# Softmax denominators summed by accumulating transfers between SBUF tiles, with two products with ones per unit in place of twelve

## The chip, the cores and the metric

One core of one Trainium2 chip. The metric is the device time of one execution in microseconds; "time" is the median of several executions, and "span" is the length of the one execution that was profiled.

In the profile PE is TensorE (the products), ACT ScalarE (here the exp and copies), DVE VectorE and POOL GpSimd (element by element; GpSimd also issues the accumulating transfers), SP the queue that issues most other transfers. A transfer **lands** when it is complete; the time to landing is counted from the start of its issue. SBUF holds the tiles, PSUM the results of products, HBM is the memory outside the core.

## The reference, cut to what matters

Eight images of 256 channels and 32 x 32 pixels go through a convolution-and-attention layer (layer 0), a channel attention and a layer of experts (layer 1). The change touches the softmax of layer 0: for each image and each of 8 heads, 1024 queries of 32 channels attend to 1426 pooled keys.

```python
# q: (8, 8 heads, 1024, 32); k, v: (8, 8 heads, 1426, 32); all float32
attn = jax.nn.softmax(jnp.einsum('bhqd,bhkd->bhqk', q_g, k) * SCALE, axis=-1)
out_att = jnp.einsum('bhqk,bhkd->bhqd', attn, v)
# ... mixing, projection, residual; then the second layer:
t = t + _L1_attn_ref(_ln_t(t), ...)
t = t + _L1_ffn_ref(_ln_t(t), ...)      # 8 experts, three matmuls each
```

## The kernel before: the parts that matter

The keys lie on the partitions: 1426 keys are eleven chunks of 128 and one of 18. A **unit** is one image, one half of the heads (four) and one half of the queries (512); there are 32. A unit has twelve **steps**, one per chunk: scores into PSUM, exp into an SBUF tile `pt` of 128 x 2048, then two groups of four products, one with the values and one with a matrix of ones, which gives the sum over the keys.

```python
def scores(b, c, sl, kc):
    ...
    pt = T(work, [P, 4, 512], "pt", bufs=2)
    f.act.activation(pt[:w], t[:w], AF.Exp, scale=SCALE0)
    return pt

def values(b, c, kc, pt, pv):
    w = KEY_CHUNKS[kc][1]
    for what in range(2):                      # 0: values, 1: ones
        for j in range(4):
            h = 4 * c + j
            lhsT = kit.ones[:w, :DH] if what else vts[b][kc // 4][:w, kc % 4, h * DH : (h + 1) * DH]
            f.pe.matmul(pv[DH * j : DH * j + DH, what, :], lhsT=lhsT, rhs=pt[:w, j, :],
                        start=kc == 0, stop=kc == NKC - 1)
```

All other work of the two attentions (convolutions, keys and values of the next image, the second layer's attention of earlier images) is written as generators, here called threads, and put between the steps. A model of each engine's clock decides at build time which thread goes next; on the chip every engine then runs in a fixed order. `PACE` is the TensorE time that background may take per step.

```python
for i in range(len(steps) + 1):
    if i < len(steps):
        ...
        pt = scores(b, c, sl, kc)
        f.step()
    if late is not None:
        ...
        values(b1, c1, kc1, pt1, pv)
        if kc1 == NKC - 1:
            ...                                # copy out, spawn normalise and project
    if i < len(steps):
        late = b, c, sl, kc, pt
        f.step(PACE)                           # 2.8 us of background
f.finish(5)
```

Of the kernel before, what the change touches and what calls it, by code (L numbers as in the profile page):

```python
# [16 lines left out]
P = 128  # L17
# [8 lines left out]
NE = 8  # L26
SCALE0 = DH ** -0.5
SCALE1 = C ** -0.5
PACE = 2.8
MARGIN = 1.5  # L30
AHEAD = {"DVE": 6.0, "ACT": 1.0, "POOL": 4.0, "SP": 10.0}
BUFS = {"sm": 2}
LIMIT = 1e12
# [610 lines left out]
class Flow:  # L644
# [18 lines left out]
    def __init__(self, tc, kit):  # L663
        nc = tc.nc
        self.tc, self.kit = tc, kit
        self.now = dict.fromkeys(("PE", "DVE", "ACT", "POOL", "SP"), 0.0)
        self.last = {}
        self.ready, self.read, self.writer, self.rings = {}, {}, {}, {}
        self.pe = self.Engine(self, "PE", nc.tensor)
        self.ve = self.Engine(self, "DVE", nc.vector)  # L670
        self.act = self.Engine(self, "ACT", nc.scalar)
        self.pool = self.Engine(self, "POOL", nc.gpsimd)
        self.sp = self.Engine(self, "SP", nc.sync)
        self.threads = []
        self.credit = 0.0

    def tile(self, pool, shape, tag, bufs=1):
        t = self.kit.tile(pool, shape, tag, bufs=bufs)
        ring = self.rings.setdefault(tag, [])
        self.ready[t.name] = self.end(ring[-bufs]) if len(ring) >= bufs else 0.0  # L680
        ring.append(t.name)
        return t

    def end(self, name):
        return max(self.ready.get(name, 0.0), self.read.get(name, 0.0))

    def free(self, tag, bufs=1):
        ring = self.rings.get(tag, [])
        return self.end(ring[-bufs]) if len(ring) >= bufs else 0.0

    def cost(self, engine, op, out, ins):
# [7 lines left out]
        if "dma" in op:  # L699
            return 0.1  # L700
# [18 lines left out]
    def note(self, engine, op, ins, args, kwargs):  # L719
# [18 lines left out]
        cost = self.cost(engine, op, out, srcs)  # L738
        self.now[engine] = end = start + cost
        lag = 3.0 if "dma" in op else 0.15  # L740
        self.ready[o] = max(self.ready.get(o, 0.0), end + lag)
        self.writer[o] = engine
# [17 lines left out]
    def runnable(self, need):  # L760
# [5 lines left out]
        if tag is not None:  # L766
            at = max(at, self.free(tag, BUFS[tag]))
        if engine == "PE":
            return not self.closed and self.credit > 0 and at + MARGIN <= pe
# [9 lines left out]
    def step(self, pace=None):  # L779
# [3 lines left out]
        if pace is not None:  # L783
            self.credit = min(self.credit + pace, 3 * pace)
# [6 lines left out]
    def finish(self, rank):  # L791

        while any(t[2] <= rank for t in self.threads):
            self.credit, self.closed = 1.0, False
            ready = [t for t in self.threads if self.runnable(t[1])]
            self.resume((ready or [t for t in self.threads if t[1][0] is not None])[0])


def attention(tc, kit, nb, x, t1, t2, hn, bounds, vecs, q_t, kv_t, proj_t, gqk_t, wqk, wqkv, vecs1, w1_d, w1c, gate_d, wrc):
# [7 lines left out]
    with ExitStack() as ctx:  # L807
# [48 lines left out]
        for t in bounds:  # L856
            f.pool.memset(t, 0.0)

# [4 lines left out]
        def mix():  # L863
# [53 lines left out]
            bd = T(wp, [P, 2, P], "bd")  # L917
# [12 lines left out]
            bdt = T(wp, [P, 2, P], "bdt")  # L930
# [26 lines left out]
        ks, qs, vts = {}, {}, {}  # L957

# [15 lines left out]
        def maps(xp, todo, done, freed):  # L974

            for m in (2, 3, 0, 1):
                c = m % 2
                yield until(lambda: len(done) >= len(todo) - 1)
                p = T(work, [P, NK], "p", bufs=2)
# [12 lines left out]
                yield until(lambda: len(todo) < 2 + 2 * len(freed))  # L992
                yield pool(p)
                acc = T(work, [P, NK], "acc", bufs=2)
                for s, n in enumerate(SIDES):
                    o = OFFS[s]
                    f.pool.tensor_scalar(
                        acc[:, o : o + n * n],
                        p[:, o : o + n * n],
                        mid[:, c * 4 + s : c * 4 + s + 1],  # L1000
                        db(c, s),
                        ALU.mult,
                        ALU.add,
                    )
                todo.append((c, p, acc))

        def convolve(todo, done):

            for m in range(4):
# [67 lines left out]
        def prepare(b, todo, done, freed):  # L1077
# [57 lines left out]
            t5 = T(work, [P, 2, 32, 5], "pool5")  # L1135
# [13 lines left out]
            yield from maps(xp, todo, done, freed)  # L1149

            for c in range(2):
                yield until(lambda: c == 0 or turn[0] >= 2 * b - 1)
                q = qs[b, c] = T(work, [P, HW], "q", bufs=3)
                for half in range(2):
# [11 lines left out]
                    f.act.activation(q[:, sl], ps, AF.Copy, scale=vec[:, V_NW + c : V_NW + c + 1])  # L1166

        def keys_and_values(b, done, freed):
            yield until(lambda: len(done) == 2)
            vts[b] = []  # L1170
            for k0 in range(0, NKC, 4):
                vt = T(work, [P, 4, C], "vt", bufs=6)
                yield from by_tokens(done[:2], vt, k0)
                vts[b].append(vt)
            freed.append(True)

            yield until(lambda: len(done) == 4)
            for k0 in range(0, NKC, 4):
                kt = T(work, [P, 4, C], "kt")
                yield from by_tokens(done[2:], kt, k0)  # L1180
                s0, w = KEY_SLICES[k0 // 4]
                for c in range(2):
                    if k0 == 0:
                        yield until(lambda: c == 0 or turn[0] >= 2 * b - 1)
# [6 lines left out]

        def ahead(b):
            todo, done, freed = [], [], []
            f.spawn(keys_and_values(b, done, freed), 1)
            f.spawn(convolve(todo, done), 2)
            f.spawn(prepare(b, todo, done, freed), 3)

        def scores(b, c, sl, kc):
# [5 lines left out]
            pt = T(work, [P, 4, 512], "pt", bufs=2)  # L1204
# [3 lines left out]
        def values(b, c, kc, pt, pv):  # L1208
            w = KEY_CHUNKS[kc][1]
            for what in range(2):  # L1210
                for j in range(4):
                    h = 4 * c + j
                    lhsT = kit.ones[:w, :DH] if what else vts[b][kc // 4][:w, kc % 4, h * DH : (h + 1) * DH]
                    f.pe.matmul(
                        pv[DH * j : DH * j + DH, what, :],
                        lhsT=lhsT,
                        rhs=pt[:w, j, :],
                        start=kc == 0,
                        stop=kc == NKC - 1,
                    )  # L1220

        def normalise(b, c, sl, av):
            yield ve(av)
            rec = T(work, [P, 512], "rec")
            f.ve.reciprocal(rec, av[:, 1, :])
            yield pool(rec)
            f.pool.tensor_tensor(atts[b, c][:, sl], av[:, 0, :], rec, ALU.mult)
            for o in (0, C):
                f.pool.tensor_tensor(hi, hi, av[:, 1, o : o + C], ALU.add)
            for o in (0, C):  # L1230
                f.pool.tensor_tensor(lo, lo, rec[:, o : o + C], ALU.add)

        def project(b):
            yield until(lambda: scored[0] >= b - 1)
            t = T(work, [P, 2, HW], "t", bufs=2)
            f.sp.dma_start(t, x[b].rearrange("(k p) n -> p k n", p=P))
            for m in range(2):
                for half in range(2):
                    sl = slice(half * 512, half * 512 + 512)
                    yield pe(atts[b, 0], atts[b, 1], tag="sm")  # L1240
# [5 lines left out]
                    yield ve(ps, t)  # L1246
                    f.ve.scalar_tensor_tensor(t[:, m, sl], ps, bias[:, m : m + 1], t[:, m, sl], ALU.add, ALU.add)
            f.sp.dma_start(t1[b], t)
            tokens.append(t)
# [36 lines left out]
        turn, scored, written, tokens, probabilities = [0], [0], [0], [], []  # L1286

        def layer1():

            for b in range(nb):  # L1290
                yield until(lambda: len(tokens) > b)
                t = tokens[b]
# [13 lines left out]
                for n in range(4):  # L1306
# [15 lines left out]
                    yield until(lambda: 4 * b + n < written[0] + 2)  # L1322
                    p1 = T(work, [P, 8, C], "p1", bufs=2)
                    for g in range(4):
                        yield pe(y, tag="sm")
                        ps = small()
                        for u in range(2):
# [9 lines left out]
                        f.act.activation(  # L1337
                            p1[:, 2 * g : 2 * g + 2, :], ps.rearrange("p (u c) -> p u c", u=2), AF.Exp, scale=SCALE1
                        )
                    probabilities.append((b, q, p1, v))  # L1340
                scored[0] += 1

        def outputs():

            for i in range(4 * nb):
                yield until(lambda: len(probabilities) > i)
                b, q, p1, v = probabilities[i]
                res = T(work, [P, 2, C], "res", bufs=2)
                f.sp.dma_start(res, t1[b][:, :, q])
                yield pool(p1)  # L1350
                s = T(work, [P, 2, C], "s")
                f.pool.tensor_tensor(s, p1[:, 0:2, :], p1[:, 2:4, :], ALU.add)
                f.pool.tensor_tensor(s, s, p1[:, 4:6, :], ALU.add)
                f.pool.tensor_tensor(s, s, p1[:, 6:8, :], ALU.add)
                f.pool.tensor_tensor(s[:, 0, :], s[:, 0, :], s[:, 1, :], ALU.add)
                f.pool.tensor_tensor(hi, hi, s[:, 0, :], ALU.add)
# [4 lines left out]
                rec = T(work, [P, C], "rec1")  # L1361
                f.ve.reciprocal(rec, ps[:, :C])
                f.pool.tensor_tensor(lo, lo, rec, ALU.add)
                yield pe(p1, v, tag="sm")
                ps = small()
                for m in range(2):
                    for kc in range(8):
                        f.pe.matmul(
                            ps[:, m * C : (m + 1) * C],
                            lhsT=v[:, kc, m * P : (m + 1) * P],  # L1370
                            rhs=p1[:, kc, :],
                            start=kc == 0,
                            stop=kc == 7,
                        )
                yield ve(ps, rec)
                o = T(work, [P, 2, C], "o", bufs=2)
# [10 lines left out]
        def centred(src, width, dst):  # L1387
# [15 lines left out]
        def weights1():  # L1403


            raw = T(work, [P, 2, 512], "p1", bufs=2)
            f.sp.dma_start(raw, wqk)
            wvr = T(work, [P, 2, C], "p1", bufs=2)
            f.sp.dma_start(wvr, wqkv.rearrange("(k p) f -> p k f", p=P)[:, :, 2 * C :])
            bqkv = T(wp, [P, 6], "bqkv")  # L1410
# [18 lines left out]
            g = T(work, [P, 2, C], "t", bufs=2)  # L1429
            f.ve.tensor_copy(g, ps.rearrange("p (m f) -> p m f", m=2))  # L1430
            yield from centred(g, C, gw)
# [558 lines left out]
```

## Time and profile before

The profiled span of 3860 us has four stages: the preparation of the first image; the **attention stage** (the 384 steps with their background), 2110 us with TensorE busy 2047; a **tail**, in which the second layer's attention of the last image ends; and the experts. Their lengths and busy times are the first lines that the prediction shows.

The time was 3864.97 us in three runs. Read the stages by TensorE's busy time: where it fills nearly the whole stage, removing its work can shorten the stage; where it does not, something else ends the waits.

### The profile page before, as it was taken

To read this page: it belongs to the slowest core of one execution; us is meant where nothing else is said; L and a number is where in the kernel's file an instruction comes from. 1 tells how busy PE (TensorE), PEld (TensorE's weight loads), DVE (VectorE), ACT (ScalarE), POOL (GpSimd) and SP (SyncE) were. 2 spreads that over 40 slices of the span, in tenths; PEclk is the share of its full clock that TensorE was granted. 3 is DMA by queue.
4 is the path that set the end of the run, shared out by engine and by line. 5 is a ranking of instruction groups with operands and counts; after the bars stand their busy time and mean duration, and the time that the engine had idled before them with its cause. 6 is when DMAs were issued, how large, how long until landed. Compare 5 with 4: busy or idle time off the path is not lost.

```text
span 3859.8 us, 40154 instructions
## 1 busy us (share of the span) xinstructions
PE 3625.5 (94%) x16666; PEld 1624.4 (42%) x16666; DVE 1389.2 (36%) x2533; ACT 1505.2 (39%) x1625; POOL 762.8 (20%) x848
## 2 busy tenths in 40 slices
PE   3499999999899899899899997799999999999999
PEld 1233344434444444444444455444444444444444
DVE  5555563846636626636522121211111111111111
ACT  1256555564454554454454421212222222222222
POOL 3132324324224224224222222100000000000000
PEclk7699999999999999999999998879999999999999
DMA  1010001000010010010000010500000000000000
GB/s 40 14 39 26 15 4 47 12 28 20 12 36 20 12 36 23 9 36 23 9 28 28 17 46 23 195 17 17 17 17 16 22 17 28 16 17 17 17 11 12
DMA packets 55296, 99.97 MB, mean 26 GB/s; under 512 B 6448, under 2 KB 31672, under 8 KB 52928
## 3 DMA queue, kind: packets, MB, share of 16 engines
q1 hardware_dynamic: 49440, 84.76, 6.3%
q0 software_dynamic: 1152, 8.39, 0.5%
q10 hardware_dynamic: 4512, 4.16, 0.3%
q8 instruction: 133, 2.18, 0.2%
q14 instruction: 59, 0.48, 0.0%
HBM read 61.64 MB, written 35.66 MB: 25 GB/s over the span
## 4 chain that ended last, share of the span: by engine, by line
PE 75%; DVE 13%; issue 4%; POOL 4%; ACT 4%; DMA 0%; ACTq 0%; POOLq 0%; DVEq 0%
PE sc L1701 23%; PE sm L657 20%; PE y L1748 12%; PE pv L657 11%; DVE acc L657 10%; PE sc L657 8%; ACT pt L657 3%; DVE rec L657 1%; POOL s L657 1%; POOL bound L657 1%; PE y L1743 1%; PE sc L1807 1%; POOL rstd L657 1%; DVE tst L657 0%; POOL acc L657 0%
## 5 line engine op out<-in xcount | busy, mean ns | idle before, releaser
L657 ACT ACTIVATE pt<-sc 128x2048 f32<-128x2048 f32 (+1 forms) x384 | 720.9, 1877 | 547.4 <-PE sc L657 546.8
L1709 ACT ACTIVATE h<-sc,bnvec 128x512 f32<-128x512 f32 x512 | 370.7, 774 | 1011.9 <-PE sc L1701 977.1
L657 DVE SCALAR_TENSOR_TENSOR acc<-p,vec,acc 128x961 f32<-128x961 f32 (+7 forms) x1024 | 628.9, 623 | 150.0 <-POOL acc L657 119.2
L1733 DVE TENSOR_TENSOR h<-h,gb 128x1024 f32<-128x1024 f32 x128 | 156.9, 1225 | 1116.1 <-ACT h L1709 1095.8
L1701 PE MATMUL sc<-hn,w1e 128*128 128x512 f32 x1024 | 462.0, 594 | 9.4 <-DVE bnvec L1676 9.4
L1748 PE MATMUL y<-h,wo 128*128 128x512 f32 x1024 | 463.6, 597 | 0.0
L1701 PE MATMUL sc<-h,w2e 128*128 128x512 f32 x1024 | 460.2, 592 | 0.0
L657 PE MATMUL sc<-q,kn 32*128 32x512 f32 (+1 forms) x3072 | 438.0, 640 | 13.4 <-ACT pt L657 13.3
L657 PE MATMUL pv<-pt,vt 128*32 128x512 f32 (+1 forms) x3072 | 409.9, 605 | 0.0
L657 PE MATMUL pv<-pt,con 128*32 128x512 f32 (+1 forms) x3072 | 399.7, 592 | 0.0
L1701 PEld LDWEIGHTS sc<-hn,w1e 128*128 128x128 f32 x1024 | 195.3, 191 | 255.0 <-issue 255.0
L1748 PEld LDWEIGHTS y<-h,wo 128*128 128x128 f32 x1024 | 194.3, 191 | 251.9 <-issue 251.7
L1701 PEld LDWEIGHTS sc<-h,w2e 128*128 128x128 f32 x1024 | 194.6, 190 | 244.9 <-issue 244.9
L657 PE MATMUL sm<-p,v 128*128 128x256 f32 x1024 | 245.2, 401 | 40.5 <-DVE rec L657 40.5
L657 ACT ACTIVATE p<-sm 128x512 f32<-128x512 f32 (+1 forms) x224 | 130.7, 584 | 364.5 <-PE sm L657 356.4
L657 PE MATMUL sm<-y,t 128*128 128x256 f32 x1024 | 243.3, 387 | 3.1 <-ACT p L657 2.7
L657 PEld LDWEIGHTS sm<-p,v 128*128 128x128 f32 x1024 | 206.7, 203 | 79.5 <-DVE rec L657 42.1
L657 POOL TENSOR_TENSOR rstd<-rstd,mhalf 128x4 f32<-128x4 f32 (+2 forms) x88 | 84.5, 960 | 749.9 <-DVE rstd L657 749.9
L657 PEld LDWEIGHTS sm<-y,t 128*128 128x128 f32 x1024 | 190.5, 191 | 73.5 <-issue 42.6
L657 PEld LDWEIGHTS pv<-pt,con 128*32 128x32 f32 (+1 forms) x3072 | 99.6, 110 | 230.9 <-issue 230.9
L657 PEld LDWEIGHTS sc<-q,kn 32*128 32x128 f32 (+1 forms) x3072 | 115.0, 176 | 193.7 <-issue 119.8
L657 PE MATMUL sm<-xp,kvw 128*128 128x512 f32 (+1 forms) x384 | 176.8, 601 | 15.1 <-DVE xp L657 6.7
(177 smaller groups left out, 2599.3 us busy)
## 6 DMA issues: line engine op xcount, KB each, us to landing
xp<-in_x_dram SPq DMA_DIRECT2D x8, 1024.0 KB, 5.8
t<-in_x_dram SPq DMA_DIRECT2D x8, 1024.0 KB, 6.8
t<-t SPq DMA_DIRECT2D x8, 1024.0 KB, 3.9
res<-t SPq DMA_DIRECT2D x32, 256.0 KB, 3.3
t<-o SPq DMA_DIRECT2D x32, 256.0 KB, 2.4
hn<-o SPq DMA_DIRECT2D x32, 256.0 KB, 2.7
hn<-hn SPq DMA_DIRECT2D x16, 512.0 KB, 4.0
t<-t SPq DMA_DIRECT2D x16, 512.0 KB, 4.0
```

Of the source, the lines that this page charges most:

```text
L657: ins = fn(*args, **kwargs)
L1701: nc.tensor.matmul(ps[:, m, :], lhsT=wt[:, e, k, m * P : (m + 1) * P], rhs=src[:, k, :], start=k == 0, stop=k == 1,)
L1709: nc.scalar.activation(dst[:, m, :], ps[:, m, :], AF.Relu, bias=col(c, e, m), scale=col(s, e, m))
L1733: nc.vector.tensor_tensor(h, h, gb[:, e : e + 1, sl].to_broadcast([P, 2, 512]), ALU.mult)
L1743: nc.tensor.matmul(y[m], lhsT=bo[:, m * P : (m + 1) * P], rhs=gt[:, sl], start=True, stop=False)
L1748: nc.tensor.matmul(y[m], lhsT=wo[:, e, k, m * P : (m + 1) * P], rhs=h[:, k, :], start=False, stop=e == NE - 1 and k == 1,)
L1807: nc.tensor.matmul(ps[:, sl], lhsT=sel[:, e * P : (e + 1) * P], rhs=gt[:, sl], start=True, stop=True)
```

## The change

The intent is to take ten of twelve products with ones off TensorE. Chunks 0 and 3 of a unit are written into tiles that stay (`sum`); every other chunk's exp tile is added into one of the two by a transfer from SBUF to SBUF that accumulates at its destination. Two products with ones per unit then sum the partitions.

```diff
+SUMS = (0, 3)
+LANDING = 8.0
+CAP = 1.5
...
-            pt = T(work, [P, 4, 512], "pt", bufs=2)
+            pt = T(work, [P, 4, 512], "sum", bufs=3) if kc in SUMS else T(work, [P, 4, 512], "pt", bufs=3)
...
+        def add(kc, pt, into):
+            w = KEY_CHUNKS[kc][1]
+            f.pool.dma_start(
+                out=into[:w].rearrange("p j q -> p (j q)"), in_=pt[:w].rearrange("p j q -> p (j q)"), accum_op=ALU.add
+            )
...
-        for i in range(len(steps) + 1):
+        for i in range(len(steps) + 5):
...
+            if due and due[0][0] == i:
+                _, part, s, av2, behind = due.pop(0)
+                ...
+                sums(part, s, total)
...
+                values(b1, c1, kc1, pt, pv)
+                if kc1 in SUMS:
+                    parts.append(pt)
+                else:
+                    add(kc1, pt, parts[kc1 % len(parts)])
...
+                    due += [(i + 3 + part, part, s, av, behind) for part, s in enumerate(parts)]
```

To pay for the tiles, the background was rewritten too (cut here): threads that run on over all images instead of being started per image, queries of later images sent through HBM, centre taps of the convolution moved from GpSimd to ScalarE, single buffers in place of pairs. The build model now knows that an add lands 8 us after its issue (`LANDING`).

## The prediction

> **What bounds the kernel now.** I read the split of the span by stage first (a busy-time table over four stretches, whose borders I took from the first score product at 178.0 us, the last sum product at 2287.7 us and the check product at 2447.5 us). Its columns are busy us and instruction counts of each engine, granted clock, DMA share, GB/s:
>
> ```profile
> 0.00:178.00 178.00, 67.32 (x176) 35.06 (x176) 100.72 (x237) 34.42 (x64) 43.90 (x55) 0.70 0.09 29
> 178.00:2288.00 2110.00, 2047.38 (x12864) 891.46 (x12864) 1050.05 (x2026) 1075.46 (x1014) 664.37 (x735) 0.99 0.07 23
> 2288.00:2447.00 159.00, 118.58 (x424) 86.86 (x420) 39.95 (x83) 16.31 (x26) 44.19 (x48) 0.86 0.11 38
> 2447.00:3860.00 1413.00, 1392.24 (x3210) 611.00 (x3210) 198.51 (x188) 379.04 (x521) 10.32 (x10) 0.98 0.08 29
> ```
>
> Preparation of the first image takes 178 us. The first attention stage takes 2110 us, with TensorE busy 97% of it and everything else at half. Then comes a tail of 159 us, in which the second layer's attention of the last image runs alone with TensorE at 75%. The experts take 1413 us and the change does not touch them. So the question is TensorE's work in the 2110 us, and the length of the tail. In the page's groups, the product with ones (`con`) costs as much as the product with the values:
>
> ```profile
> L657 PE MATMUL pv<-pt,vt 128*32 128x512 f32 (+1 forms) x3072 | 409.9, 605 | 0.0
> L657 PE MATMUL pv<-pt,con 128*32 128x512 f32 (+1 forms) x3072 | 399.7, 592 | 0.0
> ```
>
> Starts are safer than busy time, because ends are modelled. The timeline of one stretch shows a step (there are 384: 8 images x 2 channel halves x 2 query halves x 12 key chunks) with no background work in it:
>
> ```profile
> 1162.81 1.14 PE L657 MATMUL sc<-q,kn 32*128 32x512 f32 x8
> ...
> 1163.88 1.06 PE L657 MATMUL pv<-pt,vt 128*32 128x512 f32 x8
> 1164.07 1.88 ACT L657 ACTIVATE pt<-sc 128x2048 f32<-128x2048 f32 x1 [0.96 <-PE sc L657]
> ...
> 1164.76 1.04 PE L657 MATMUL pv<-pt,con 128*32 128x512 f32 x8
> ...
> 1166.00 1.14 PE L657 MATMUL sc<-q,kn 32*128 32x512 f32 x8 [0.20 <-ACT pt L657]
> ```
>
> Scores take 1.07 us to the next start, values 0.88. Ones take 0.97 to the next group where nothing waits (1154.41 to 1155.38 in the same timeline). Together 2.92 us. The bare step lasts 3.19 (the next one, 1166.00 to 1169.24, 3.24), because one score tile exists and the next scores wait for the exp: **a floor of 3.2 us a step**. The mean step is 2110/384 = 5.5 us, so it holds some 2.6 us of background products and TensorE is the bound on average.
>
> **What the Trainium skill says.** (1) "TensorE: Matmul & The Clock Gate", Part 3 (packing small matmuls): products in different column groups run concurrently. The trace agrees: eight records of 592 ns each leave 0.88 us between group starts. (2) "DMA: Bandwidth & Descriptors", SWDGE vs HWDGE vs iDMA: an accumulating transfer can only be issued from GpSimd. The kernel before has none, so its trace cannot say what one costs. (3) Same page, Rules for kernel authors: an accumulate reads its destination and writes it later, and must wait for the earlier one's semaphore. Hence the adds into one tile form a serial chain. (4) "Collectives: The Full Stack", The bandwidth ceiling: an add runs at about half a copy's rate because it needs two source reads. No run here shows it yet. For the copy rate I use the trace:
>
> ```profile
> q0 software_dynamic: 1152, 8.39, 0.5%
> feat<-hn POOLq DMA_DIRECT2D x7, 1024.0 KB, 8.3
> ```
>
> 0.5% of 16 engines' 3860 us is 309 us for 8.39 MB: 27 GB/s an engine, 434 GB/s for sixteen. Halved, 217 GB/s.
>
> **The change, part by part.** I read the listing of each engine's instructions in program order for both kernels.
>
> *Ones products.* 384 groups of 0.88 us go. 32 units (an image, channel half and query half) x 2 groups of 0.97 come. Foreground work: 384 x 2.92 = 1121 us before; 384 x 2.04 + 64 x 0.97 = 783 + 62 = 845 after. **276 us saved.**
>
> *Background products.* I priced each at 0.90 us per 512 columns plus 0.03 (462.0 us for the 512 products behind the 1024 records of the experts' first product), small ones at 0.2. Before, 1023 us of them lie between the score groups. Each step as the larger of 3.2 and 2.92 + its background, with the price scaled by 0.954, gives 2114 us: the measured 2110, so this pricing is calibrated. The same on the new order gives **1752 us**, from 861 x 0.954 = 821 us of background, 845 of foreground and 88 of waits at the floor (112 steps are below it; before 64 steps, 17 us). So the stage loses 358 us: 276 of ones, 155 because background moved behind the last unit, less 71 of new floor.
>
> *The tail.* That moved work is not free. In the new order three images' second-layer value projections come after the last score group; before, one. In the trace before, an image there takes from 2331.2 (value projection) to 2445.5 (last scaling product), and 19 us more for its statistics:
>
> ```profile
> 2331.20 8.99 PE L657 MATMUL sm<-wv,t 128*128 128x256 f32 x32
> ...
> 2354.03 0.70 PE L657 MATMUL sm<-s,con 128*128 128x256 f32 x2 [2.89 <-POOL s L657]
> ...
> 2445.54 1.22 PE L657 MATMUL sm<-diag,con 128*128 128x256 f32 x2 [3.26 <-POOL diag L657]
> ```
>
> The four waits of 2.9 us for `s` should mostly go, since the new order puts score products of the next tile between. I take 105 + 113 + 120 for the three, 17 for the last adds, sums and reciprocal, 8 for the projection: **363 us instead of 159**.
>
> *The adds.* Ten a unit: nine of 128 x 2048 (1.05 MB) and one of 18 rows. At 217 GB/s a full one occupies the DMA engines 4.83 us (estimate from the Collectives page and the row above), so a unit needs 9 x 4.83 + 1 = 44.5 us and has 1752/32 = 54.8: 81% busy. Two of the 32 units are shorter than that, so about 5 us are lost. Two chains alternate, so a chain adds every two steps, 9.1 us on average. The change's own model reckons 8 us to landing, which just fits; three `pt` buffers allow about three steps between exp and landing. I count 5 us.
>
> *Others.* GpSimd loses the centre taps and the bound sums (128 + 192 instructions in the listing) and gets 320 issues; ScalarE gets the taps and the accumulating copies, some 115 us by the page's 584 to 774 ns for such sizes. At (1075 + 115)/1757 it is 68% busy: not a bound. VectorE has 1050 us in 1757, 60%. Preparation: the taps' wait on GpSimd goes, one `p` buffer costs it back; 178 us.
>
> Sum: 178 + 1757 + 363 + 1413 = 3711 us of span; the timed median was about 5 us above the profiled span, so **3715 us**, 4% faster.
>
> **Rivals.** *DMA becomes the bound.* If an add occupies 6 us rather than 4.83, a unit needs at least 55 us and the same sum over units gives about 1840 us of stage, hence about 3800 us (1.7% faster); at 7 us, 64 us a unit, about 2050 and 4010 us. For it: 90% of the DMA engines' time is near saturation once the other 7% of traffic is added, and no trace line shows an accumulate. Against it: the change keeps two partial sums and short chains, as someone would who had timed it. *GpSimd held up.* Each add waits in GpSimd's queue for the add before it into the same tile; powers, pooling and sums behind it come late, and TensorE waits for `sm` operands. This would cost perhaps 0.2 us a step, 77 us: about 3790. *The tail is shorter or the floor absent.* Had the background stayed within the steps, 204 us of tail would be traded for 155 of TensorE work: about 3665; finer `p1` tiles may bring part of it.
>
> **Range and chances.** The certain term is the 276 us; the order fixes the tail to within some 40 us; the adds can only cost. The low end, 3630, is a tail of 300 us and a little less background; the high end, 3860, is adds of about 6.2 us or GpSimd delay with the tail as computed. A gain of over 2% needs less than 3788. I give 0.76 faster, 0.18 within 2%, 0.06 slower.
>
> **What would show it.** Right: `con` products in the attention stage fall from 3072 records to 512; the last score group starts near 1930 us; the tail to the check lasts 330 to 390 us with TensorE at about 75%; the software queue moves some 315 MB with a share that gives about 4.8 us an add; score products wait mainly on exp. Wrong: TensorE or exp waiting on `sum` or `pt` transfers for over 50 us in all, landings well above 10 us, `sm` products waiting on GpSimd, or a last score group after 2020 us.

## The result

The changed kernel took 4184.74 us (4166.92 to 4189.83, four runs) against 3864.12 (3861.19 to 3869.66, four runs): a ratio of 1.0816, 95% interval 1.0786 to 1.0847, **8% slower**, where 4% faster was predicted. The ratios are not quite those of the medians that are quoted. Both kernels' outputs pass the comparison with the reference (what that is worth is said under the experiments).

The same split by stage, for the kernel after (window, its length, then busy us and instruction counts of PE, PEld, DVE, ACT and POOL, the granted clock, the DMA engines' share, GB/s):

```profile
0.00:172.00 172.00, 66.93 (x181) 35.41 (x182) 101.55 (x248) 45.41 (x86) 21.12 (x39) 0.67 0.10 30
172.00:2388.00 2216.00, 1775.94 (x9643) 715.83 (x9646) 972.36 (x1917) 1141.70 (x1312) 611.73 (x720) 0.90 0.78 167
2388.00:2752.00 364.00, 282.19 (x1080) 212.20 (x1072) 85.81 (x185) 56.69 (x124) 79.11 (x80) 0.87 0.12 38
2752.00:4165.10 1413.10, 1393.49 (x3208) 611.71 (x3208) 197.73 (x185) 379.04 (x521) 9.54 (x9) 0.98 0.08 29
```

TensorE lost 271 us of busy time in the attention stage (2047 to 1776), nearly as planned, and the stage still became 106 us longer (2110 to 2216): TensorE now stands idle for 440 us of it, no other engine is busier than 52%, and only the DMA engines come near it, at 0.78. The tail grew from 159 us to 359 (2388 to the check product at 2747). The borders of the stages are good to some 4 us. What is waited for stands in the page of the kernel after (queue lines: packets, MB, share of 16 engines; group lines: count, busy us, mean ns, idle time before them and its releaser; last line: KB and median us to landing):

```profile
q0 software_dynamic: 44160, 315.12, 37.6%
...
L662 ACT ACTIVATE pt<-sc 128x2048 f32<-128x2048 f32 x320 | 600.1, 1875 | 526.9 <-DMA sum<-pt 284.4
...
L662 PE MATMUL sc<-q,kn 32*128 32x512 f32 (+1 forms) x3072 | 484.7, 703 | 180.4 <-ACT pt L662 177.7
...
L662 POOL DMA_DIRECT2D sum<-pt x320 | 281.4, 892 | 1054.2 <-DMA sum<-pt 531.0
...
sum<-pt POOLq DMA_DIRECT2D x288, 1024.0 KB, 9.5
```

Read from the bottom: an add lands 9.5 us after its issue. GpSimd waits 531 us for the add before into the same tile; of the 160 adds that had one before them in a unit's first tile, 100 began within 1 us of its landing, and none before it. ScalarE waits 284 us with the next exp, because no `pt` buffer is free until the add that reads it has landed. TensorE waits 178 us for exp, because one score tile exists. Before the change the last wait was small. TensorE's waits in the attention stage (us in all, times, longest), kernel before:

```profile
PE sm L657 <- DVE rec L657: 40.5, 4, 10.3
PE sc L657 <- ACT pt L657: 13.3, 58, 0.6
```

and kernel after:

```profile
PE sc L662 <- ACT pt L662: 177.7, 113, 8.2
PE sm L662 <- DVE xr L662: 97.7, 18, 11.2
PE sm L662 <- ACT kt L662: 27.0, 11, 6.3
PE sm L662 <- DVE mv L662: 23.1, 4, 14.6
```

All TensorE waits for background operands (`sm`) add up to 245 us there, against 49 before. The largest of them is for `xr`, the residual that the projection adds to; experiment 1 comes back to it. A stretch of the timeline shows one stall passed on (start, length, instruction, in brackets the idle time before it and what ended it):

```profile
1407.83 1.88 ACT L662 ACTIVATE pt<-sc 128x2048 f32<-128x2048 f32 x1 [4.54 <-DMA sum<-pt]
1408.26 0.92 POOL L662 DMA_DIRECT2D sum<-pt  x1 [2.45 <-DMA sum<-pt]
1409.76 2.09 PE L662 MATMUL sc<-q,kn 32*128 32x512 f32 x8 [4.82 <-ACT pt L662]
...
1413.93 1.88 ACT L662 ACTIVATE pt<-sc 128x2048 f32<-128x2048 f32 x1 [4.23 <-DMA sum<-pt]
1414.37 0.86 POOL L662 DMA_DIRECT2D sum<-pt  x1 [5.19 <-DMA sum<-pt]
...
1415.86 1.14 PE L662 MATMUL sc<-q,kn 32*128 32x512 f32 x8 [1.10 <-ACT pt L662]
```

The exp at 1407.83 waits for a landing, and the scores wait for that exp. A second price follows: after idling 4.82 us, the same eight products take 2.09 us instead of 1.14. The Trainium skill, "TensorE: Matmul & The Clock Gate", Part 1 (the HAM clock gate), says that the array falls back to half its clock after an idle window of about 3.4 us. This trace agrees: from 1407.9 to 1414.6 us the granted clock was 0.50, and over the stage it fell from 0.99 to 0.90.

### The profile page after: what moved, and what is told of

The parts are those of the page before. It is cut to its first block, busy times and chain, and to the rows that moved or that the text cites. A ratio compares the mean times of both kernels' runs of the same rounds, so it can differ in the third digit from the quotient of the medians.

```text
span 4165.1 us, 36021 instructions
## 1 busy us (share of the span) xinstructions
PE 3518.6 (84%) x14106; PEld 1575.1 (38%) x14106; DVE 1357.4 (33%) x2533; ACT 1622.8 (39%) x2042; POOL 721.5 (17%) x848
## 3 DMA queue, kind: packets, MB, share of 16 engines
q0 software_dynamic: 44160, 315.12, 37.6%
## 4 chain that ended last, share of the span: by engine, by line
PE 46%; DMA 13%; issue 8%; DVE 6%; POOL 4%; ACT 3%; SPq 0%; POOLq 0%; ACTq 0%; DVEq 0%
PE sc L1781 21%; PE y L1828 11%; PE sm L662 9%; DMA sum<-pt 7%; DVE acc L662 4%; PE sc L662 2%; DMA t<-xr 2%; DMA xr<-in_x_dram 2%; PE pv L662 2%; ACT pt L662 1%; POOL s L662 1%; DMA t<-t 1%; PE y L1823 1%; POOL rstd L662 1%; PE sc L1887 1%
## 5 line engine op out<-in xcount | busy, mean ns | idle before, releaser
L662 ACT ACTIVATE pt<-sc 128x2048 f32<-128x2048 f32 x320 | 600.1, 1875 | 526.9 <-DMA sum<-pt 284.4
L662 DVE SCALAR_TENSOR_TENSOR acc<-p,vec,acc 128x961 f32<-128x961 f32 (+7 forms) x1024 | 607.2, 600 | 203.2 <-ACT acc L662 172.9
L662 PE MATMUL sc<-q,kn 32*128 32x512 f32 (+1 forms) x3072 | 484.7, 703 | 180.4 <-ACT pt L662 177.7
L662 POOL DMA_DIRECT2D sum<-pt x320 | 281.4, 892 | 1054.2 <-DMA sum<-pt 531.0
L662 PE MATMUL pv<-pt,vt 128*32 128x512 f32 (+1 forms) x2560 | 371.2, 654 | 2.5 <-ACT pt L662 2.5
L662 PEld LDWEIGHTS sc<-q,kn 32*128 32x128 f32 (+1 forms) x3072 | 125.4, 192 | 422.5 <-ACT pt L662 282.7
L662 PE MATMUL sm<-xp,kvw 128*128 128x512 f32 (+1 forms) x384 | 190.0, 635 | 86.9 <-ACT acc L662 49.5
L662 PEld LDWEIGHTS pv<-pt,vt 128*32 128x32 f32 (+1 forms) x2560 | 52.0, 111 | 279.0 <-issue 275.6
```

The costliest lines, as they stand in the source:

```text
L662: ins = fn(*args, **kwargs)
```

## The experiments

All were timed in three rounds beside the kernel before, which took 3862 to 3865 us in them. The diffs are against the kernel after unless said otherwise. "The sum" is the prediction's step sum, done again on each kernel's own order of instructions, an estimate; the **excess** is the measured attention stage less this sum. For the kernel after it is 2216 - 1753 = 463 us. All twelve kernels passed the comparison with the reference, those with wrong denominators too, so the comparison says nothing about denominators, the kernel after's included.

### 1. The adds' size: 16 of 2048 columns

```diff
-                out=into[:w].rearrange("p j q -> p (j q)"), in_=pt[:w].rearrange("p j q -> p (j q)"), accum_op=ALU.add
+                out=into[:w, 0, 0:16], in_=pt[:w, 0, 0:16], accum_op=ALU.add
```

The order of instructions on all engines is unchanged; the sums are wrong on purpose.

> Same instructions in the same order on every engine as in the changed kernel, and the same 320 accumulating transfers with the same waits, but each moves 16 instead of 2048 columns (results wrong on purpose). Theory A (the bytes of the adds: 5 us of all DMA engines each, 9.5 us to landing, held up by three pt buffers and two serial chains): landing falls to 2 to 3 us, waits on sum transfers vanish, the first attention stage falls from 2216 to about 1760 us, the run to about 3720 us. Theory B (the new thread order itself: GpSimd blocked in order, single buffers for the residual tile and the query stage): stage stays above 2100 us, run above 4050 us. A mixture: in between, and the part that stays is B's.

Measured: 3823.24 us, ratio 0.9898 (0.9881 to 0.9914): the mixture of the two theories. The stage, the software queue and two of TensorE's waits in the stage:

```profile
168.00:2043.00 1875.00, 1678.30 (x9666) 690.80 (x9667) 976.82 (x1926) 1140.24 (x1314) 612.18 (x720) 0.97 0.14 35
```

```profile
q0 software_dynamic: 44160, 10.81, 2.5%
```

```profile
PE sc L662 <- ACT pt L662: 99.4, 101, 3.9
PE sm L662 <- DVE xr L662: 6.6, 4, 2.4
```

So 361 of the 470 us between prediction and result come with the adds' bytes, and 108 do not: the stage is 1875, an excess of 122. The bytes cost 341 us of stage. 98 of these are TensorE's own products becoming slower: it is busy for 1678 us here and 1776 in the kernel after, with the same number of products within 0.3%, at a clock of 0.97 against 0.90. The other 243 are waits, most of them on two paths. Those for exp grew by 78 us (99 to 178). Those for `xr` grew by 91 (7 to 98), and no add stands in that path: `xr` has one buffer, which each image's projection fills four times by an ordinary transfer, and within an image a fill is issued when the store before it has landed (within 0.5 us, in all 17 cases that the traces of both runs have). That is a second row of landings: the 24 fills and 24 stores whose landing was traced took 252 us in the kernel after and 129 here. So the adds' bytes also act by slowing other transfers. And a bound on the whole idea: even with adds that cost next to nothing, this order of work is 1% faster than the kernel before, not 4%.

### 2. Half the columns

```diff
+                out=into[:w, 0:2].rearrange("p j q -> p (j q)"), in_=pt[:w, 0:2].rearrange("p j q -> p (j q)"), accum_op=ALU.add
```

> As the run with 16 columns, but each add moves 1024 of 2048 columns (results wrong on purpose), in the same order. Theory A: an add occupies the DMA engines 2.6 us and lands in about 5 us, less than the 8 us that the order was made for, so nearly no waits: stage 1780 to 1850 us, run 3740 to 3810 us. If the fixed part of landing (not bytes) held things up: less than a third of the 459 us comes back, run above 4030 us. Theory B: no change, about 4180 us.

Measured: 3910.66 us, ratio 1.0119 (1.0102 to 1.0136); stage 1969, excess 216; an add landed in 4.7 us at a queue share of 21.6%. Neither theory's number came: nearly no waits had been expected, 3740 to 3810 us. Of the 341 us of stage, the first half of the bytes brings 94 and the second half 247: not proportional, as where a wait outgrows its slack.

### 3. All bytes, but a copy in place of an add

```diff
-... in_=pt[:w].rearrange("p j q -> p (j q)"), accum_op=ALU.add
+... in_=pt[:w].rearrange("p j q -> p (j q)")
```

> Same order and bytes as the changed kernel, but the transfers overwrite instead of adding (results wrong on purpose). If the cost is the second read that an add needs, a transfer occupies the engines about 2.5 us instead of 5.0 to 5.3 and the run is like the one with half the columns, about 3740 to 3810 us. If the add has no cost over a copy from GpSimd, the occupancy stays near 5 us and the run near 4180 us.

Measured: 3918.78 us, ratio 1.0155 (1.0135 to 1.0176). Its page:

```profile
q0 software_dynamic: 44160, 315.12, 21.1%
...
sum<-pt POOLq DMA_DIRECT2D x288, 1024.0 KB, 4.8
```

The same 315.12 MB take 21.1% of the engines' time and not 37.6%, and land in 4.8 us and not 9.5. The stage (1970) is the half adds' to within 1 us, with twice their bytes but the same share and the same landing. So bytes as such are not the cost; the time of the transfer is. (An issue holds GpSimd for 560 ns with copies and 908 with half adds; as the stages are equal, that is not the cost either.) The time expected was missed all the same, 3740 to 3810 us, as with the half adds. Adding instead of copying costs 266 us of time (4184.74 - 3918.78). The share agrees in size with what the prediction took from "Collectives: The Full Stack", The bandwidth ceiling, where it is said of ring steps between ranks (a reduce at about half the rate of a copy); the reason given there, two source reads, no run here shows. From 8.39 MB of other traffic at 19 us of all engines, a full add occupies them (0.376 x 4165 - 19)/292.5 = 5.3 us and a copy (0.211 x 3917 - 19)/292.5 = 2.8 us, a factor of 1.9. (292.5 is the number of full adds that the remaining bytes make.)

This does not tell two explanations apart: that the DMA engines are full (throughput), or that adds stand in a row (latency). The next runs do.

### 4. One chain in place of two

```diff
-SUMS = (0, 3)
+SUMS = (0,)
...
+            pt = T(work, [P, 4, 512], "sum", bufs=2) if kc in SUMS else T(work, [P, 4, 512], "pt", bufs=4)
```

All eleven adds go into one tile, with one more `pt` buffer, one `sum` buffer fewer and one product group with ones fewer. (Its step sum: 1693 us.)

> One partial sum instead of two (results right): 11 adds a unit, all in one serial chain, two sum buffers and four pt buffers in the same memory, 32 sums groups instead of 64. No two adds overlap any more, so this also measures an add alone. Theory 'chain' (an add waits for the one before it into the same tile): an add alone lands in about 7 us, 11 of them and their issues take at least 80 us a unit, so a first attention stage of 2600 us or more and a run above 4700 us. Theory 'occupancy' (the DMA engines are simply used up, 5.2 us an add): 10% more bytes, stage about 2300 us, run about 4350 us with the longer tail of this order. Theory 'ring' (exp waits for one of three pt buffers): a fourth buffer helps, run below 4250 us.

Measured: 5234.08 us, ratio 1.3546 (1.3523 to 1.3568); stage 3089, excess 1396. Its page, then GpSimd's timeline:

```profile
q0 software_dynamic: 48768, 348.68, 33.2%
...
L662 POOL DMA_DIRECT2D sum<-pt x352 | 307.0, 886 | 1979.8 <-DMA sum<-pt 1568.9
...
sum<-pt POOLq DMA_DIRECT2D x320, 1024.0 KB, 7.0
```

```profile
1514.89 0.86 POOL L662 DMA_DIRECT2D sum<-pt  x1 [6.68 <-DMA sum<-pt]
...
1522.40 0.85 POOL L662 DMA_DIRECT2D sum<-pt  x1 [6.53 <-DMA sum<-pt]
1529.88 0.85 POOL L662 DMA_DIRECT2D sum<-pt  x1 [6.62 <-DMA sum<-pt]
```

This is the clearest run. The DMA engines are less loaded than in the kernel after (33.2% of the span; 0.61 of the stage against 0.78), each add lands sooner (7.0 us), and the kernel is 25% slower: 873 us more of stage, and 190 more of tail (550 us), since this order leaves more background for it. Adds into one tile start 7.5 us apart, one landing and 0.5 us, although each occupies the engines for only (0.332 x 5227 - 19)/324.5 = 5.3 us. Throughput cannot explain it; the row of landings does. TensorE waits for it on two paths here: 529 us for exp, and 290 for the chain's end itself, when the products with ones come up in its fixed order.

### 5. No chain: pairs

```diff
-SUMS = (0, 3)
+SUMS = (0, 2, 4, 6, 8, 10)
...
-                    add(kc1, pt, parts[kc1 % len(parts)])
+                    add(kc1, pt, parts[-1])
+                    due.append((i + 4, len(parts) - 1, parts[-1]))
```

Each odd chunk is added to the even one before it, and six product groups with ones are done per unit. No add waits for another.

> Six partial sums a unit, each of two chunks: six adds instead of ten (five full ones), none waits for another, 192 sums groups on TensorE instead of 64 (results right). Step sum for this order: 1872 us of stage and 226 us of products behind it. Theory 'bytes and chains': half the bytes and no chain leave a loss like that of the run with half columns, so stage 1980 to 2060 us, tail about 315, run 3880 to 3960 us. If GpSimd's order or single buffers were the cause: above 4050 us.

Measured: 3911.39 us, ratio 1.0124 (1.0107 to 1.0141), 6.5% below the kernel after although TensorE has four more groups per unit to do. Stage 2005, excess 133. Its page:

```profile
q0 software_dynamic: 25728, 180.90, 22.9%
...
sum<-pt POOLq DMA_DIRECT2D x160, 1024.0 KB, 7.3
```

Its GpSimd waits in the list of waits:

```profile
POOL sum L662 <- ACT pt L662: 785.0, 99, 16.3
```

GpSimd's adds now wait for exp and no longer for one another. Compare with the half adds: the DMA engines are used more (22.9% against 21.6%), landings are longer (7.3 us against 4.7), and yet the excess is 133, within 11 us of the tiny adds' 122, where the half adds had 216. Two cautions. Half of the exps go into `sum` tiles, so the three `pt` buffers are under less pressure: exp waited 57 us for a landing with the half adds and not at all here. And TensorE has more to do (a sum of 1872 us against 1753), and a busier TensorE covers more waits, as experiment 8 will show; so part of the fall from 216 to 133 may be cover. The DMA engines' load did not become free either: TensorE waited 47 us for `xr`, against 7 with tiny adds.

### 6. Chains of two: triples

```diff
-SUMS = (0, 3)
+SUMS = (0, 3, 6, 9)
...
+                    add(kc1, pt, parts[-1])
+                    if kc1 % 3 == 2:
+                        due.append((i + 4, len(parts) - 1, parts[-1]))
```

> Four partial sums a unit, each of three chunks: eight adds (seven full), chains of two, 128 sums groups (results right). Step sum 1800 us of stage, 260 us of products behind it. Theory 'chains and bytes': between pairs (six adds, no chain: 3911 us) and the change (ten adds, chains of six and four: 4184 us) although TensorE has 62 us less to do than with pairs: 3940 to 4060 us. If only the long chains mattered and two adds in a chain are free: 3860 to 3910 us.

Measured: 4066.64 us, ratio 1.0524 (1.0506 to 1.0541), 7 us above the range for chains and bytes and far from that for two free adds; stage 2121, excess 321; landing 7.4 us, queue share 30.3%. GpSimd waited 462.6 us for adds before, nearly as long as in the kernel after, while exp waited only 22 us for a landing (284 there). So a large excess does not need the shortage of `pt` buffers. Between the pairs and the kernel after in every respect: the longer the chain, the larger the excess (133, 321, 463 for chains of one, two and six adds), while the bytes grow too (181, 248, 315 MB).

### 7. A build model that expects 12 us to landing

```diff
-LANDING = 8.0
+LANDING = 12.0
```

The changed kernel's own model reckoned 8 us; the trace showed 9.5. If an order made for adds that are too fast were to blame, a larger number should help.

> Only the number by which the schedule reckons an add's landing goes from 8 to 12 us, so the fixed order of background work is made for adds as slow as they are (results right). If the loss came from an order made for faster adds: the stage falls below 2100 us and the run below 4130 us, although this order leaves 320 instead of 261 us of products for the tail. If it came from the adds themselves: the stage stays within 60 us of 2216 and the run is at or above 4184 us.

Measured: 4306.6 us, ratio 1.1143 (1.1125 to 1.1162): 3% slower than the kernel after, as the second theory said. The stage grew to 2269 and the tail to 455. The model only chooses which background goes where; it does not make a landing shorter, and it put more background behind the last unit. An order that allows for slower adds is no cure, so the belief of 8 us is not the cause; values between 8 and 12 were not tried.

### 8. The new threads without the adds

```diff
-                if kc1 in SUMS:
-                    parts.append(pt)
-                else:
-                    add(kc1, pt, parts[kc1 % len(parts)])
...
+                w1 = KEY_CHUNKS[kc1][1]
+                for j in range(4):
+                    f.pe.matmul(
+                        total[DH * j : DH * j + DH, :], lhsT=kit.ones[:w1, :DH], rhs=pt[:w1, j, :],
+                        start=kc1 == 0, stop=kc1 == NKC - 1,
+                    )
...
```

> The threads of the change alone: no adds; every chunk goes through the ones product on TensorE as in the kernel before. The step sum that gave 2110 us for the kernel before gives 2036 us of stage for this order; 181 us of products come after the last score group (between 107 before and 261 in the changed kernel), so a tail of about 250 us. Sum 172 + 2036 + 250 + 1413 = 3871 us: about the time before if theory A holds. Theory B: TensorE waits on residual, stage and GpSimd tiles as in the changed kernel, and the run is above 4000 us.

Measured: 3901.52 us, ratio 1.0106 (1.0089 to 1.0123). Stage and tail:

```profile
168.00:2228.00 2060.00, 1997.59 (x12573) 837.04 (x12572) 989.99 (x1976) 1163.98 (x1355) 366.46 (x423) 0.98 0.10 33
2228.00:2482.00 254.00, 189.63 (x727) 142.38 (x725) 62.91 (x136) 38.02 (x84) 56.01 (x57) 0.86 0.11 38
```

The rewritten threads alone lose 39 us: the stage is about 50 us shorter and the tail 93 longer, because background moved behind the last unit. The sum gave 2036 for the stage (excess 24) and 250 for the tail. So the prediction's pricing of the order holds where TensorE is the bound. With the same threads and TensorE relieved of the ones (experiment 1) the excess is 122. No run separates two explanations: waiting which a busy TensorE had covered, or what remains of the adds when they are tiny, since their 320 issues still hold GpSimd for 916 ns each and wait there for exp (599 us) in front of its other work.

### 9. The centre taps back on GpSimd, with tiny adds

What makes the 122? One theory: the taps moved to ScalarE delay exp. The edit gives them back to GpSimd, on top of experiment 1:

```diff
-                            f.act.activation(acc[:, a:z], ps[:, a - s0 : z - s0], AF.Identity, bias=..., scale=...)
+                    f.pool.tensor_scalar(acc[:, o : o + n * n], p[:, o : o + n * n], mid[...], db(c, s), ALU.mult, ALU.add)
```

> As the run with adds of 16 columns (results wrong on purpose), but the convolution's centre taps go back from ScalarE to GpSimd, as in the kernel before; the step sum for this order is 1757 us (1753 for the other). It tells what the 118 us are by which the run with 16 columns stayed above the predicted stage. If ScalarE, on which the change puts the taps between the exps, makes them: the stage falls from 1875 by 50 us or more, run below 3775 us. If the taps are not it: within 25 us of 3823 us.

Measured: 3852.26 us, ratio 0.9961 (0.9944 to 0.9978): 29 us slower than experiment 1, not faster, and so just outside both ranges. That theory fell. In experiment 1 TensorE waits 102 us for exp and 91 for operands of background products (26 for `kt`, 21 for `acc`, the rest in small parts); the sum held 88 for the floor of a step, and its calibration on the kernel before held that kernel's 49 for operands. The 57 left of these are half of the 122. No one operand carries the rest, and it stays unsettled.

### 10. Adds on VectorE instead of transfers

The pairs of experiment 5 with

```diff
-            f.pool.dma_start(out=..., in_=..., accum_op=ALU.add)
+            f.ve.tensor_tensor(into[:w], into[:w], pt[:w], ALU.add)
```

> As the run with pairs, but VectorE adds the pairs (2.3 us for 128x2048 by the timed rows of the experts; 192 x 2.3 = 440 us more on VectorE, 1420 of some 1950) and no accumulating transfer is left (results right). Step sum 1880 us of stage, 228 us of products in the tail. If only the transfers made the pairs slow: 40 to 100 us faster than the pairs by transfer, 3820 to 3900 us. If VectorE becomes the bound or delays the taps: slower than those.

Measured: 3969.69 us, ratio 1.0270 (1.0253 to 1.0288); stage 2070, excess 190, 58 us slower than the pairs by transfers. At one add per two chunks the transfer is the better adder: its chain is gone, and it leaves VectorE alone (busy 976 us of the stage with transfers, 1410 with VectorE's adds).

### 11. The old threads with adds on VectorE

The kernel before, with VectorE adding pairs and six ones-products per unit (`res` and `o` became single, and three small tiles share the memory of others, to make room).

```diff
-            pt = T(work, [P, 4, 512], "pt", bufs=2)
+            pt = T(work, [P, 4, 512], "pt", bufs=3)
...
+        def add(kc, pt, into):
+            w = KEY_CHUNKS[kc][1]
+            f.ve.tensor_tensor(into[:w], into[:w], pt[:w], ALU.add)
```

> The kernel before with its own threads, but VectorE adds the chunks in pairs (192 adds of 2.3 us) and TensorE makes six ones products a unit instead of twelve; a third pt buffer, paid for with single buffers for four small tiles (results right). Step sum 1929 us of stage (2114 for the kernel before), 192 us of products behind it (107). 178 + 1929 + 265 + 1413 = 3785 us without new waits; with 30 to 60 us of waits on VectorE 3815 to 3845 us, 1% faster than before. If VectorE's adds delay the taps as in the run with pairs on VectorE in the new threads: 3900 us or more.

Measured: 4262.49 us, ratio 1.1031 (1.1013 to 1.1049); stage 2377, tail 293. A miss. Each add stands in VectorE's fixed order and waits there for exp, 426 us in all, and VectorE's work for the background waits behind it. TensorE waits 142 us for these adds when the sums come up. The run tells nothing of the transfers; it shows that this order does not go with adds.

### 12. The pairs with more background in the steps

Experiment 5 left 316 us of tail. Its edit on top:

```diff
-PACE = 2.8
-CAP = 1.5
+PACE = 3.4
+CAP = 3.0
```

> The pairs by accumulating transfers (six adds a unit, none waiting for another add, six ones-products), with the background paced more evenly: PACE 3.4 and CAP 3.0 in place of 2.8 and 1.5, so that less background is left behind the last unit. The sum over the listing's steps gives 2004 us of attention stage and 93 us of TensorE work behind it (pairs_dma: 1872 and 226). Theory: the six adds cost no more here than the 133 us that pairs_dma's stage was longer than its sum, and the tail becomes about 145 us instead of 316; then 170 + 2137 + 145 + 1413 = 3865, the same as the kernel before. If the adds' cost shrinks because a longer stage leaves the transfers more time (excess 60 us or less), the time is 3790 or below and the version beats both. If the background that comes late costs more than pairs_dma's, it is over 3900 us.

Measured: 3885.65 us, ratio 1.0061 (1.0044 to 1.0078). Stage and tail:

```profile
170.00:2319.00 2149.00, 1956.90 (x11378) 842.18 (x11377) 1030.30 (x2036) 1179.21 (x1393) 564.09 (x643) 0.97 0.51 113
2319.00:2472.00 153.00, 104.71 (x380) 75.30 (x374) 35.09 (x73) 19.77 (x44) 28.22 (x28) 0.80 0.12 40
```

The tail fell to 153 us as reckoned, and the excess stayed (2149 - 2004 = 145). So it is not the tail that keeps the pairs behind: work moved from the tail into the stage, at the same price. This is the best version found with correct sums, 7% below the kernel after, and still 0.6% above the kernel before: no version with correct sums beat that one.

| kernel | us | adds per unit | longest chain | landing, us | queue share | excess, us |
|---|---|---|---|---|---|---|
| after | 4184.7 | 10 | 6 | 9.5 | 37.6% | 463 |
| copy, not add | 3918.8 | 10 | 6 | 4.8 | 21.1% | 217 |
| half adds | 3910.7 | 10 | 6 | 4.7 | 21.6% | 216 |
| tiny adds | 3823.2 | 10 | 6 | 2.0 | 2.5% | 122 |
| one chain | 5234.1 | 11 | 11 | 7.0 | 33.2% | 1396 |
| triples | 4066.6 | 8 | 2 | 7.4 | 30.3% | 321 |
| pairs | 3911.4 | 6 | 1 | 7.3 | 22.9% | 133 |
| ones again | 3901.5 | 0 | | | 0.5% | 24 |

## Why the prediction was wrong

**The ones-products: right.** In the kernel after, the products with ones (`total<-sum,con`) are 512 records where there were 3072. TensorE's busy time in the stage fell by 271 us, even at a lower clock.

**The background's price and the tail: right.** 359 us of tail against 363 predicted, with TensorE at 78% of its window; and in experiment 8 the stage came within 24 us of the sum.

**The adds: wrong, and this decided it.** The failed step is "so a chain adds every two steps, 9.1 us on average. The change's own model reckons 8 us to landing, which just fits; ... I count 5 us." The term of 5 us measured 341 in the stage (the kernel after less the tiny adds). The prediction's own signs of being wrong came: exp waited 284 us on `sum` transfers, and the last score group began at 2372 us, not near 1930. Three things were wrong in it.

- Its sizes were optimistic, though not wildly: 5.3 us of engine time per add instead of 4.83 (the copy's rate came from a share of 0.5%, given to one digit), and 9.5 us to landing instead of 8. An add that was issued with none in flight landed in 7.0 us (94 adds), one with another in flight in 10.2 (187): the second chain lengthens the first one's links.
- It held two averages against each other. The first tile takes six adds, not five, so its unit has five waits in a row. One link is a landing and 0.5 us until the next issue begins, 10.0 us at 9.5; five are 50, an estimate from measured parts. In the trace the first to the sixth add took 44 to 78 us, in the median 52, and from the sixth to the next unit's first add passed 4 us at the least and 12.5 in the median. So no unit, from first add to first add, was shorter than 56 us (42 with tiny adds), where the mean was to be 54.8. Nothing could absorb a delay, and the steps come unevenly: many are at the floor of 3.2 us, so that two of them are 6.4 us, well under a landing.
- It did not follow a late landing to its end. An add that is late holds GpSimd (531 us), it holds a `pt` buffer and so exp (284 us), exp holds the scores (178 us), and then TensorE runs its next products at half clock (98 us over the stage). Background operands come late as well (245 us of waits against 49), of which `xr` has 98, since its own transfers land later; the others were not followed up.

The DMA rival came nearer and was still wrong in its kind. At 5.3 us per add it gives less than its 3800 us for 6 us. The engines are indeed full in dense stretches, but with the engines less loaded a longer chain cost 873 us of stage (experiment 4). That a row of latencies binds is shown there; in the kernel after it is shown for most links of the first tile (100 of 160). The engines' load has a part too, by longer landings and by the waits for `xr`, and ten unchained adds per unit, which would show its size, were not run. The rival "GpSimd held up" named part of the mechanism, with 77 us where it was hundreds.

**A term left out: 108 us.** With adds of 16 columns the time was 3823, not 3715. The sum let TensorE wait only at the floor of a step. With TensorE relieved, late operands come into sight; whether its work had covered them or the tiny adds' issues make them is not shown. Half of it can be pointed to in the waits; the rest is open.

**The sum of it.** 3715 predicted, +108 that stay with tiny adds, +96 for the bytes as copies, +266 for adding instead of copying: 4185.

**What stays open.** How the adds' cost in the kernel after is shared between the chain, the load on the DMA engines and the shortage of `pt` buffers. A fourth buffer would tell of the last, but the kernel does not build with its 8 KB more per partition. The triples had a large excess with next to no such shortage, and in experiment 4 a fourth `pt` buffer did not save the long chain.

## What to carry to other kernels

An accumulating transfer into one tile is a link in a chain: price it by its time to landing plus the half microsecond until the next one starts, times the links in a row, and not by the bytes over the bandwidth. Compare that row with the shortest stretch of work it must hide in, not with the mean, and ask which buffer stays taken until it lands and which other transfers it holds up. And when the bound engine is relieved, run the change with its new cost made tiny first: here that run would have shown that 1% was all there was to win with this order.

## What the Trainium skill lacked or had wrong

- "DMA: Bandwidth & Descriptors": gives no time for an accumulating transfer from SBUF to SBUF. For 128 x 2048 float32: 7.0 us from issue to landing with one in flight, 10.2 when another is in flight at its issue, 9.5 over all in the kernel after; 5.3 us of all 16 engines' time. The plain copy: 4.8 and 2.8 us.
- The same page tells to wait for the earlier accumulate's semaphore (Rules for kernel authors), and not what the wait costs: one link every 7.5 us in the one-chain run, against 5.3 us by throughput, and 1370 us over the kernel before.
- No page says that issuing an accumulate holds GpSimd longer than issuing the same copy: 892 ns against 560 ns per issue for the same tiles, and 916 ns when it moves 16 columns only.
- "Collectives: The Full Stack" has the rate of a reduce at about half a copy's for ring steps between ranks; for adds between tiles of one core it has none, and the runs show a factor of 1.9. Nothing that a page states was found wrong.
